# A two-layer graph network on one core: the turned blocks of the attention matrix move from place to place on chip, in halves of a row, instead of through DRAM

## The chip, the core and the metric

The kernel runs on one core of a Trainium2 chip. The core has a matrix engine (TensorE, in the profile PE, with its weight loads as PEld), a vector engine (VectorE, DVE), an engine for functions (ScalarE, ACT), a general engine (GpSimd, POOL) and a queue engine (SyncE, SP) that here issues nearly all DMAs. Sixteen DMA engines do the transfers. The metric is the time of one execution on the device in microseconds (us), median of several runs; lower is better.

## The reference, cut to what matters

There are N = 3327 nodes with 256 features, and a sparse weighted matrix `adj` (3327 x 3327). Layer 0 does two steps of a bilinear attention and of a plain propagation, and layer 1 is an attention over the neighbours with four heads:

```
h = relu(layernorm(x))
# layer 0
R = adj + I;  R = R / R.sum(-1)
Xf = Xa = h;  Z = 0
for n in 0, 1:
    P  = softmax((Xa W1' W2') (Xa W3')')      # 3327 x 3327, dense
    A  = P, in each row the largest entries up to a sum of 0.9, normalised
    Xf = R @ Xf;  Xa = A @ Xa
    Z += Xf @ U1[n]' + Xa @ U2[n]'
x = x + layernorm(h + Z) * g + b
# layer 1
hp = relu(layernorm(x)) @ W                    # 4 heads of 64
e  = leaky_relu(s_i + d_j) where adj > 0, else -inf
x  = x + elu(softmax(e) @ hp)
```

All is float32. The dense product `A @ Xa` is the part that the change touches.

## The kernel before, in words

Nodes are cut into 26 tiles of 128 (3328 places). Layer 0 goes through the 26 tiles of rows twice (steps n = 0 and 1); "a row" below means such a row of tiles, 128 x 3328 numbers called `e`. Layer 1, the neighbour stage, goes over four blocks of 832 columns, and in each over the 26 tiles.

What happens to one row of `e`:

- `logits` (L904) are PE products into PSUM, and `exps` (L919 to L922) writes their exponentials to `e`. It stores them so that each group of 256 columns holds two tiles interleaved.
- `count` (L956) on ScalarE, `before` and `step` on GpSimd (L960 to L1004) search the threshold of the 0.9. `window` (L1014, L1019), `sort` and `choose` on VectorE settle it.
- `drop` (L1070) on VectorE clears what lies below it, in three pieces of 1024, 1024 and 1279 columns.
- `A @ Xa` needs `e` transposed as the stationary operand. `turn_blocks` (L1082) transposes each 32 x 32 block in place with VectorE's stream transpose, piece by piece, three a row. The blocks then have to change places. `put_blocks` (L1086) writes a piece to the DRAM tile `blocks`, and `get_blocks` (L1091) reads it back with block row and block column exchanged, four DMAs a piece, one for each 32 partitions. So a row has 3 puts and 12 gets.
- `attend_blocks` (L1098) makes the 26 products into the PSUM tile `acca`, and `attended` (L1102) scales them out on ScalarE. `finish1` or `finish2` then projects the result for the next step, or closes layer 0 and prepares layer 1.

Beside this runs the full product `R @ Xf` (class `Full`, L1117 loads, L1123 products): seven loads of `adj` a tile (the tile `at`, four buffers), 26 products into `accf`. In layer 1 `load` (L1678) fetches `adj`, `mask` (L1688, L1689) makes a 0/1 mask from it on ScalarE, `exponents` (L1700) on VectorE the unnormalised attention, and `product` (L1716) and `sums` (L1730) on PE the results.

The order of the work is written by a planner. Every piece of work is a `plan.put(engine, length, rank, function, needs=..., take=..., give=..., lag=...)`: the engine that issues it, a time in us, a rank (the lower goes first), what it waits for, which buffers it takes and gives back, and how long after it its result may be used. `Plan.order` plays this through with one queue for each engine, and the program is issued in the order that comes out. On the chip each engine then works off its own list in that fixed order, and semaphores hold it where a result or a buffer is not there yet. The numbers of buffers stand in the dictionary handed to `Plan` and in `BUFS`: `e` 4 and `e5` 1 (a row of `e` in the tile `qq`, for 10 of the 52 rows), `et` 3 and `f` 3. `attention` and `search` set up the pieces of a row. VectorE's turn and SP's moves have ranks just below that row's; full products of step 0 have the rank 2 + 1.3 t for tile t, those of step 1 have 31 + t.

Small users of the buffers that the change touches: `weights`, `layer1_loads`, `layer1_scores`, the copies in `stats` (L826) and the masks use `et`; `Full.copy`, `Full.take` and the fetch of x1 (L1822) use `f`.

Of the kernel before, what the change touches and what calls it, by code (L numbers as in the profile page):

```python
# [10 lines left out]
F32 = mybir.dt.float32  # L11
# [4 lines left out]
ALU = mybir.AluOpType  # L16
# [31 lines left out]
PART = 1024  # L48
PIECE_AT = [PART * (k // 5) + 205 * (k % 5) for k in range(PIECES)] + [N]
# [4 lines left out]
BUFS = dict(kk=2, e=4, sc=6, f=3, xa=2, xt=2, kq=3, ystage=2, base=1, mv=4, cum=2)  # L54
# [532 lines left out]
def fast(  # L587
# [58 lines left out]
    with ExitStack() as l0:  # L646
# [5 lines left out]
        etpool = l0.enter_context(tc.tile_pool(name="etpool", bufs=3))  # L652
# [17 lines left out]
        blocks = spill.tile([NT // 2, P, 2 * P], F32, name="blocks")  # L670
# [27 lines left out]
        def weights():  # L698
            held = {}
            w1 = etpool.tile([P, 4, P], F32, name="et")  # L700
# [49 lines left out]
        def layer1_loads():  # L750
# [4 lines left out]
            a_all = etpool.tile([P, H, 2 * FH], F32, name="et")  # L755
# [4 lines left out]
            return g_all, b_all, wa, a_all  # L760

        def layer1_scores(wa, a_all):

            prod = etpool.tile([P, 2, H, FH], F32, name="et")
            for k in range(2):
                for a in range(2):
                    V.tensor_mul(
                        prod[:, 0],
                        wa[:, k, : H * FH].rearrange("p (h f) -> p h f", h=H),
                        a_all[:, :, a * FH : (a + 1) * FH],  # L770
                    )
                    lo = H * FH + a * H
                    V.tensor_reduce(wa[:, k, lo : lo + H], prod[:, 0], AX.X, ALU.add)
# [35 lines left out]
        def stats(n, lo, hi, rank, needs, scaled):  # L809
# [13 lines left out]
            def copy(held, m):  # L823
                qg = etpool.tile([P, 4, P], F32, name="et").rearrange("p a b -> p (a b)")
                held["qg"] = qg[:, : 3 * (2 * DA + 1)].rearrange("p (a b) -> p a b", a=3)
# [11 lines left out]
            for t0 in range(lo, hi, 2):  # L837
                held, m = {}, min(2, hi - t0)
                a = plan.put("PE", 0.25 * m, rank, product, held, t0, m, needs=[needs, scaled], take=["px"])
                a = plan.put("ACT", 0.45, rank, copy, held, m, needs=[a], take=["et"], give=["px"])  # L840
                ends.append(plan.put("DVE", 0.35 * m + 0.2, rank, square, held, t0, m, needs=[a], give=["et"]))
# [23 lines left out]
        plan = Plan(dict(rows=1, mvs=3, pl=2, px=2, acca=1, accf=1, et=3, at=4, y=1, e2=2, ec=1, mask=2, e5=1, qg=2, **BUFS))  # L865
# [4 lines left out]
        class Row:  # L870
# [7 lines left out]
            def __init__(self, n, i):  # L878
                self.n, self.i, self.pl, self.pt, self.et = n, i, {}, {}, {}
# [197 lines left out]
            def part(self, g):  # L1077
                return self.e[:, g * PART : (g + 1) * PART if g < 2 else NP]

            def turn_blocks(self, g):  # L1080
                part = self.part(g).rearrange("p (g s t) -> p g t s", s=P, t=2)
                V.transpose(part, part)  # L1082

            def put_blocks(self, g):
                src = self.part(g).rearrange("p (g w) -> p g w", w=2 * P)
                nc.sync.dma_start(blocks[4 * g : 4 * g + src.shape[1]].rearrange("g p w -> p g w"), src)  # L1086

            def get_blocks(self, g, o):
                to = self.part(g)[o * P // 4 : (o + 1) * P // 4].rearrange("p (c w) -> p c w", w=P // 2)
                src = blocks[4 * g : 4 * g + to.shape[1] // 4, :, o * P // 2 : (o + 1) * P // 2]  # L1090
                nc.sync.dma_start(to, src.rearrange("g (b s) w -> s (g b) w", b=4))  # L1091

            def attend_blocks(self, js):
                for j in js:
                    if j == 0:
                        self.acc = ps_a.tile([P, D], F32, name="acca")
                    lhs = self.e[:, j // 2 * 256 : (j // 2 + 1) * 256].rearrange("p (q t) -> p t q", t=2)[:, j % 2, :]
# [420 lines left out]
        def attention(row, rank, total, drops, right):  # L1518
            a = None
            come = []  # L1520
            for g in range(3):
                b = plan.put(
                    "DVE", 1.17 if g < 2 else 1.44, rank - 1.001, row.turn_blocks, g, needs=[drops[g]]
                )
                b = plan.put("SP", 0.5, rank - 1.0, row.put_blocks, g, needs=[b], lag=8.0)
                b = plan.put("", 0.0, -90.0, lambda: None, needs=[b], lag=0.0)
                come.append(
                    [plan.put("SP", 0.6, rank - 1.0, row.get_blocks, g, o, needs=[b], lag=5.5) for o in range(4)]
                )
            for j in range(0, NT - 2, 4):  # L1530
                js = range(j, j + 4 if j < 20 else NT)
                a = plan.put(
                    "PE", 0.432 * len(js), rank, row.attend_blocks, js, needs=[come[j // 8], a, right],
                    take=["acca"] * (j == 0), give=[own_e[row.n][row.i]] * (j == 20),
# [28 lines left out]
        def attend_neighbours(rows, ends, done, fulls):  # L1563
# [80 lines left out]
            for b in range(4):  # L1644
# [14 lines left out]
                for j in range(NT):  # L1659
# [22 lines left out]
                    def mask(held=held, off=off):  # L1682
                        m = etpool.tile([P, 4, P], F32, name="et").rearrange("p a b -> p (a b)").bitcast(BF16)
                        m = held["mask"] = m[:, :W]
# [54 lines left out]
                    own = ["et", "mask"]  # L1739
                    if b == 0 and j < 2:  # L1740
                        loads, own = plan.put("SP", 0.2, rank, load_first, needs=[opened[0]], lag=4.0), []
                        m_ = plan.put("ACT", 1.8, rank, mask_first, needs=[loads])
# [198 lines left out]
        for n in range(STEPS):  # L1941
# [30 lines left out]
            if n == 0:  # L1972
# [21 lines left out]
                def layer1():  # L1994
# [7 lines left out]
                    "DVE", 3.7, base + 5.0, lambda: layer1_scores(late["wa"], late["a"]), needs=[a], take=["et"],  # L2002
                    give=["et", "et"],
# [75 lines left out]
```

## Time and profile before

| | us |
|---|---|
| three runs | 2112.4, 2110.24, 2112.68; median 2112.4 |
| the profiled execution | 2112.06 |
| its span, first to last instruction | 2110.3 |
| PE busy | 2033.4 |
| VectorE busy | 1693.6 |
| ScalarE busy | 1297.6 |
| GpSimd busy | 1028.4 |

| from the page | |
|---|---|
| mean granted clock of PE | 0.992 |
| packets, bytes, mean rate | 637551, 361.61 MB, 171 GB/s |
| share of the DMA engines taken by SP's queue | 72.8% |
| bytes read from HBM, and written | 254.39 MB, 104.58 MB |
| puts `blocks<-e` and `blocks<-qq` | 84 + 20 of 512 KB, 42 + 10 of 640 KB |
| gets `e<-blocks` and `qq<-blocks` | 336 + 80 of 128 KB, 168 + 40 of 160 KB |

The profile is of one execution. A busy time counts the time in which an engine had an instruction of its own at work; waiting and issuing DMAs are not in it, so SP has no busy time of its own, and its DMAs are listed with the time that their issue took. Matmuls overlap, and a busy PE need not be PE at its peak. The span falls into a start (to about 100 us), step 0 (to about 780 us), step 1 (to about 1630 us) and the neighbour stage with the output (to 2110 us). Where the waits of an engine are listed, the name behind the arrow is the instruction or DMA whose end came last before the engine went on.

### The profile page before, as it was taken

How to read it: one execution, taken by the hardware profiler on the slowest of the kernel's cores; microseconds unless marked ns; L12 is line 12 of the kernel's file. 1: busy time of each engine (PE TensorE's matmuls, PEld its weight loads, DVE VectorE, ACT ScalarE, POOL GpSimd, SP SyncE). 2: the span in 40 equal slices, each digit the busy share in tenths (PEclk: the TensorE clock that was granted, in tenths of full speed). 3: DMA queues.
4: the chain of work that ended last, by engine and by line, in shares of the span. 5: the costliest groups of instructions: out<-in, count | busy, mean ns of one | idle time of the engine just before them, and what ended most of it. 6: DMA issues, size and time to landing. Idle time of an engine off the chain costs nothing. (4 is left out here: it accounts for less than half of the span.)

```text
span 2110.3 us, 33982 instructions
## 1 busy us (share of the span) xinstructions
PE 2033.4 (96%) x10519; PEld 1398.5 (66%) x10519; DVE 1693.6 (80%) x3768; ACT 1297.6 (61%) x2630; POOL 1028.4 (49%) x2222
## 2 busy tenths in 40 slices
PE   8999999999999889999999999999888999999997
PEld 6477778777787777778878787777776333333332
DVE  5579899887987734788778888888787989999894
ACT  4776685577656307873777777776552447464642
POOL 4367676566665404777577767777672000000001
PEclk9999999999999999999999999999999999999999
DMA  3189889888888975999879898887899444444340
GB/s 95 52 190 212 187 199 216 187 199 190 191 207 180 216 174 161 195 211 220 171 180 200 180 215 188 197 202 175 187 231 203 120 132 138 132 136 119 117 123 27
DMA packets 637551, 361.61 MB, mean 171 GB/s; under 512 B 373706, under 2 KB 590320, under 8 KB 637360
## 3 DMA queue, kind: packets, MB, share of 16 engines
q1 hardware_dynamic: 636464, 359.13, 72.8%
q8 instruction: 86, 1.41, 0.3%
q14 instruction: 105, 0.86, 0.1%
q10 hardware_dynamic: 896, 0.21, 0.0%
HBM read 254.39 MB, written 104.58 MB: 170 GB/s over the span
## 5 line engine op out<-in xcount | busy, mean ns | idle before, releaser
L1098 PE MATMUL acca<-rhs,e 128*128 128x256 f32 x2184 | 489.6, 381 | 18.1 <-DMA e<-blocks 7.0
L956 ACT ACTIVATE junk<-e,sc 128x3327 fp8e5<-128x3327 f32 x147 | 450.8, 3066 | 54.4 <-POOL sc L993 53.0
L1098 PEld LDWEIGHTS acca<-rhs,e 128*128 128x128 f32 x2184 | 425.6, 197 | 70.3 <-issue 13.8
L1123 PE MATMUL accf<-main,at 128*128 128x257 f32 x1352 | 322.2, 387 | 13.0 <-DMA at<-in_adjt_dram 6.7
L1123 PE MATMUL accf<-c,at 128*128 128x256 f32 x1352 | 311.8, 385 | 17.4 <-DMA at<-in_adjt_dram 9.0
L1123 PEld LDWEIGHTS accf<-main,at 128*128 128x128 f32 x1352 | 252.0, 192 | 75.2 <-issue 18.3
L1123 PEld LDWEIGHTS accf<-c,at 128*128 128x128 f32 x1352 | 254.7, 192 | 69.6 <-DMA at<-in_adjt_dram 11.9
L1019 DVE MAX8 cands<-y 128x8 f32<-128x205 f32 (+1 forms) x832 | 242.7, 361 | 3.7
L1014 DVE SCALAR_TENSOR_TENSOR y<-e,sc 128x1639 f32<-128x1639 f32 x84 | 167.3, 1991 | 68.2 <-POOL sc L1004 67.1
L1879 POOL TENSOR_TENSOR qq<-qq 128x256 f32<-128x256 f32 x4 | 2.9, 728 | 432.6 <-ACT qq L1875 432.6
L1716 PE MATMUL pl<-e,main 128*64 128x416 f32 x1024 | 191.6, 517 | 0.0
L1689 ACT ACTIVATE et<-at 128x448 bf16<-128x448 f32 (+1 forms) x204 | 112.2, 550 | 127.6 <-DVE e L1700 71.7
L919 ACT ACTIVATE e<-pl 128x1024 f32<-128x1024 f32 x126 | 137.6, 1099 | 65.7 <-PE pl L904 64.1
L904 PE MATMUL pl<-kt,qg 64*128 64x512 f32 (+1 forms) x832 | 173.7, 536 | 2.8 <-ACT e L919 2.8
L1082 DVE STREAM_TRANSPOSE e<-e 128x1024 f32<-128x1024 f32 (+1 forms) x126 | 168.6, 1338 | 7.1 <-POOL sc L993 0.5
L1070 DVE SCALAR_TENSOR_TENSOR e<-e,thr 128x1024 f32<-128x1024 f32 (+1 forms) x126 | 171.0, 1357 | 1.5 <-issue 0.4
L1716 PEld LDWEIGHTS pl<-e,main 128*64 128x64 f32 x1024 | 69.3, 137 | 110.5 <-issue 95.7
L1688 ACT ACTIVATE at<-at 128x448 f32<-128x448 f32 (+1 forms) x204 | 110.6, 542 | 45.3 <-DMA at<-in_adjt_dram 44.0
L1700 DVE SCALAR_TENSOR_TENSOR e<-c,low,et 128x832 f32<-128x832 f32 x128 | 129.4, 1070 | 8.1 <-issue 6.2
L1700 DVE SCALAR_TENSOR_TENSOR e<-qq,low,et 128x832 f32<-128x832 f32 x120 | 121.8, 1077 | 10.6 <-ACT et L1689 3.8
L904 PEld LDWEIGHTS pl<-kt,qg 64*128 64x128 f32 x832 | 71.4, 186 | 88.1 <-issue 74.7
L1102 ACT ACTIVATE xa<-acca,sc 128x256 f32<-128x256 f32 x52 | 24.2, 466 | 158.3 <-PE acca L1098 158.3
(547 smaller groups left out, 3436.6 us busy)
## 6 DMA issues: line engine op xcount, KB each, us to landing
at<-in_adjt_dram SPq DMA_DIRECT2D x414, 256.0 KB
blocks<-e SPq DMA_DIRECT2D x84, 512.0 KB
e<-blocks SPq DMA_DIRECT2D x336, 128.0 KB
blocks<-e SPq DMA_DIRECT2D x42, 640.0 KB
e<-blocks SPq DMA_DIRECT2D x168, 160.0 KB
at<-in_adjt_dram SPq DMA_DIRECT2D x102, 192.0 KB
blocks<-qq SPq DMA_DIRECT2D x20, 512.0 KB
qq<-blocks SPq DMA_DIRECT2D x80, 128.0 KB
```

Source lines behind the costliest of these rows:

```text
L904: T.matmul(pl[:, lo : lo + m], qg[self.n, self.i // 4][half, self.i % 4, :], kt[half, 512 * k : 512 * k + m], start=True, stop=True,)
L919: S.activation(to, pl.rearrange("p (g t q) -> p g t q", g=4, t=2), AF.Exp, accum_out=sums[k])
L956: S.activation(junk[:, :N], self.e[:, :N], fn, bias=t, scale=-1.0, accum_out=dst, saturate=False)
L1014: V.scalar_tensor_tensor(self.y[:, : hi - lo], self.e[:, lo:hi], self.up, self.e[:, lo:hi], ALU.is_lt, ALU.mult, accum_out=(self.h0, self. ...
L1019: V.max(self.cands[:, a * PIECES // 2 + k, :], self.y[:, at[k] - lo : at[k + 1] - lo])
L1070: V.scalar_tensor_tensor(piece, piece, self.thr[:, at : at + 1], piece, ALU.is_gt, ALU.mult)
L1082: V.transpose(part, part)
L1098: T.matmul(self.acc, lhs, rhs[self.n][:, j, :], start=(j == 0), stop=(j == NT - 1))
L1123: T.matmul(self.acc[:, : self.w], self.at[j // JC][:, j % JC, :], self.src[:, j, : self.w], start=(j == 0), stop=(j == NT - 1),)
L1689: S.activation(to, src, AF.Sign)
L1700: V.scalar_tensor_tensor(held["e"][:, k, :], extra["both"][b % 2][:, k, :], low[:, j, k : k + 1], held["mask"], ALU.max, ALU.mult,)
L1716: T.matmul(q["acc"][a][k * FH : (k + 1) * FH, c, :C], main[:, j, h * FH : (h + 1) * FH], held["e"][:, h, c * C : (c + 1) * C], start=(j == 0),
```

## The change

- VectorE turns a row's blocks in two halves, of 1792 and 1536 columns, in place of three pieces. The first half follows the second drop, the second the third.
- The DRAM tile `blocks`, the puts and the gets are gone. A new buffer of 128 x 1792 (the tile `et`, now one buffer of that size in place of three of 512 columns) takes the first half: `move(0, q)` issues four DMAs, which carry the blocks of 32 source partitions to four places in it. `move(1, q)` then carries the second half into the columns of `e` where the first half stood: four DMAs, all into the same 32 partitions. A row has 32 such DMAs, each of 32 partitions with 7 or 6 runs of 256 bytes.
- `attend_blocks` reads the first 14 tiles from `et` and the last 12 from the front of `e`. Its pieces are cut accordingly; the piece with tiles 12 and 13 gives `et` back.
- The small users of `et` go elsewhere: the copies of `stats` take an `f` buffer, masks take the tile `junk` (two places, the same two `mask` tokens as before), and layer 1's `a` and the products made from it share the one `et`. `f` has two buffers in place of three.

The core of the diff:

```diff
-BUFS = dict(kk=2, e=4, sc=6, f=3, xa=2, xt=2, kq=3, ystage=2, base=1, mv=4, cum=2)
+BUFS = dict(kk=2, e=4, sc=6, f=2, xa=2, xt=2, kq=3, ystage=2, base=1, mv=4, cum=2)
...
-        etpool = l0.enter_context(tc.tile_pool(name="etpool", bufs=3))
+        etpool = l0.enter_context(tc.tile_pool(name="etpool", bufs=1))
...
             def copy(held, m):
-                qg = etpool.tile([P, 4, P], F32, name="et").rearrange("p a b -> p (a b)")
-                held["qg"] = qg[:, : 3 * (2 * DA + 1)].rearrange("p (a b) -> p a b", a=3)
+                qg = small.tile([P, H * FH + 2 * H], F32, name="f", bufs=BUFS["f"])
+                held["qg"] = qg[:, : 2 * (2 * DA + 1)].rearrange("p (a b) -> p a b", a=2)
...
+            def half(self, h):
+                return self.e[:, h * HALF : HALF if h == 0 else NP]
+
+            def turn_blocks(self, h):
+                half = self.half(h).rearrange("p (g s t) -> p g t s", s=P, t=2)
+                V.transpose(half, half)
+
+            def move(self, h, q):
+                if (h, q) == (0, 0):
+                    self.first = etpool.tile([P, HALF], F32, name="et")
+                src = self.half(h).rearrange("p (g o w) -> p g o w", o=4, w=P // 2)
+                to = (self.e if h else self.first)[:, : src.shape[1] * 2 * P]
+                to = to.rearrange("p (g b w) -> p g b w", b=4, w=P // 2)
+                for k in range(4):
+                    o, b = (k, q) if h == 0 else (q, k)
+                    nc.sync.dma_start(to[o * 32 : (o + 1) * 32, :, b, :], src[b * 32 : (b + 1) * 32, :, o, :])
...
-                    lhs = self.e[:, j // 2 * 256 : (j // 2 + 1) * 256].rearrange("p (q t) -> p t q", t=2)[:, j % 2, :]
+                    g = j // 2 * 2 * P
+                    lhs = self.first[:, g : g + 2 * P] if g < HALF else self.e[:, g - HALF : g - HALF + 2 * P]
+                    lhs = lhs.rearrange("p (q t) -> p t q", t=2)[:, j % 2, :]
...
-            for g in range(3):
-                b = plan.put(
-                    "DVE", 1.17 if g < 2 else 1.44, rank - 1.001, row.turn_blocks, g, needs=[drops[g]]
-                )
-                b = plan.put("SP", 0.5, rank - 1.0, row.put_blocks, g, needs=[b], lag=8.0)
-                b = plan.put("", 0.0, -90.0, lambda: None, needs=[b], lag=0.0)
-                come.append(
-                    [plan.put("SP", 0.6, rank - 1.0, row.get_blocks, g, o, needs=[b], lag=5.5) for o in range(4)]
-                )
+            for h in range(2):
+                b = plan.put("DVE", 1.98 if h == 0 else 1.72, rank - 1.001, row.turn_blocks, h, needs=[drops[h + 1]])
+                a, own = b, []
+                for q in range(4):
+                    a = plan.put(
+                        "SP", 1.55, rank - 1.0, row.move, h, q, needs=[b, a, come[0][q] if h else None], take=["et"] * (h + q == 0), lag=3.5
+                    )
+                    own.append(a)
+                come.append(own)
...
-                    def mask(held=held, off=off):
-                        m = etpool.tile([P, 4, P], F32, name="et").rearrange("p a b -> p (a b)").bitcast(BF16)
-                        m = held["mask"] = m[:, :W]
+                    def mask(j=j, held=held, off=off):
+                        m = held["mask"] = extra["m"][:, j % 2, :]
...
-                    own = ["et", "mask"]
+                    own = ["mask"]
```

## The prediction, made before the changed kernel was run

> **What bounds the kernel now.** I read the page's busy times first, then the slices, then stretches of the span, and last what TensorE (PE) waits for.
>
> ```profile
> PE 2033.4 (96%) x10519; PEld 1398.5 (66%) x10519; DVE 1693.6 (80%) x3768; ACT 1297.6 (61%) x2630; POOL 1028.4 (49%) x2222
> ...
> PEclk9999999999999999999999999999999999999999
> DMA  3189889888888975999879898887899444444340
> ```
>
> PE is busy for 2033.4 of 2110.3 us. Its instructions do not change, so whatever the change gains has to come out of the 77 us in which PE is idle, and a little from the clock (0.992 granted on the mean). The DMA digits show the second thing that is nearly full: through both attention steps (about 100 to 1620 us) the 16 engines are 80 to 90% busy. The stretches of the span tell where the idle time of PE lies (columns: length, then busy time of PE, weight loads, VectorE, ScalarE, GpSimd; granted clock; DMA share; GB/s):
>
> ```profile
> 200.00:300.00 100.00, 99.48 (x459) 77.88 (x459) 89.09 (x233) 68.82 (x129) 69.24 (x138) 1.00 0.93 201
> ...
> 700.00:760.00 60.00, 51.17 (x224) 42.02 (x225) 39.75 (x110) 12.79 (x16) 16.92 (x38) 0.98 0.92 199
> ...
> 1400.00:1500.00 100.00, 94.56 (x437) 75.43 (x434) 82.84 (x219) 72.92 (x145) 70.73 (x156) 1.00 0.82 186
> 1500.00:1600.00 100.00, 88.59 (x383) 73.68 (x382) 81.66 (x186) 45.63 (x84) 67.50 (x128) 0.95 0.88 201
> ```
>
> In the middle of step 0 PE is full (3.6 us idle from 200 to 700). It idles 13 us where step 0 ends (700 to 800), 7 us from there to 1000, 13.5 us from 1000 to 1500, 17 us from 1500 to 1650, and 22 us in the first 200 us and the last 110 us, which the change does not touch. What PE waited for over the whole span (us in total, times, longest):
>
> ```profile
> PE accf L1123 <- DMA at<-in_adjt_dram: 15.7, 8, 3.8
> PE acca L1098 <- DMA e<-blocks: 7.0, 11, 1.5
> PE accf L1123 <- ACT main L1137: 5.6, 3, 2.9
> PE acca L1730 <- ACT xa L1102: 4.0, 1, 4.0
> ...
> PE acca L1098 <- DMA qq<-blocks: 1.2, 3, 0.4
> ```
>
> So 23.9 us of the idle time ended with a DMA: 15.7 with a load of adj for the full product, 8.2 with the way through DRAM itself. The rest ended with ScalarE, VectorE and GpSimd, which the change leaves as they are. From about 1650 us on DMA is under half busy and PE has no idle time until 2060; no gain is to be had there.
>
> **What goes: the way through DRAM.** A row of e has 3328 columns. Three puts (L1086) write it in 128 x 13 = 1664 packets of 1 KB, twelve gets (L1091) bring it back in 128 x 52 = 6656 packets of 256 B. The trace's packet records, grouped by size, give 52 ns for a 1 KB packet and 28 ns for a 256 B one (5th to 95th percentile 18 to 47). Over 16 engines that is 1664 x 52 / 16 = 5.4 us for the puts and 6656 x 28 / 16 = 11.7 us for the gets. Rows follow each other every 25.5 us in step 0 (first transposes of row 0 at 102.1, of row 25 at 740.8) and every 29.9 us in step 1 (843.6 and 1592.1). At a share of 0.89 the engines work 22.7 us a row in step 0; the two kinds are 17.1 of them, so all else is 5.6.
>
> The new 32 moves are again 6656 packets of 256 B. No row shows such a packet read on chip. I take the same 28 ns, since the write side is the same (32 partitions, 256 B runs), and keep 18 and 47 ns as ends: 7.5 to 19.6 us a row. With 28 ns a row is 5.6 + 11.7 + 0.2 (17 more completions on 16 engines of 12 ns) = 17.5 us of 25.5: the share falls from 0.89 to about 0.69. That is the gain's source, and its size: a get took 0.9 us of all engines (512 x 28 / 16), a move takes 0.4, so an adj load queued behind them waits half as long.
>
> **What comes: issues on SyncE's queue (SP).**
>
> ```profile
> L1091 SPq DMA_DIRECT2D e<-blocks x504: 303/507/3138, 110.1 to 1616.4; - x168
> L1086 SPq DMA_DIRECT2D blocks<-e x126: 359/377/1047, 103.3 to 1604.0; - x126
> ```
>
> Median issue is 0.38 us for a put and 0.51 for a get, the means 0.39 and 0.70. In the queue's records the DMAs count on eight semaphores in turn, and a long issue is one that waits for the DMA eight places earlier: the get at 321.84 us takes 2.2 us, until the one issued at 316.74 has landed, 7.3 us after its issue. So the surplus over the median is the full engines' doing and shrinks with them. A row's 15 issues cost 9.5 us of SP now, and 0.05 us between each. For a move I take 0.42 us, between the put and the uncongested get; ends 0.33 (an adj load's lower rows) and 0.70. 32 x (0.42 + 0.05) = 15.0 us against 9.5 + 0.8 = 10.3. SP's DMAs fill 53.9% of 200 to 700 us, 13.7 us a row, so the rest is 4.2 (4.5 with the gaps), and SP goes to 19.5 of 25.5 us, 77%. It is not full, but what queues behind a blocked move (the adj loads, which feed the full products) has less room. The plan books 1.55 us for four moves, 0.39 each, so SP will run late against it. I price this at +6 us over 52 rows, from 0 to +45.
>
> The moves wait for the turned half (VectorE), and the first of a row for the single buffer that the first half's products (PE) must have left. Behind that move in SP's queue stand adj loads. The buffer is held for 16 moves (7.5 us), a landing (2 to 3 us) and 14 tiles at 0.45 us (6.3): some 17 us of a 25.5 us row, so it decides nothing unless PE comes 8 us late, and then PE is busy. The second half's moves wait for the first half's reads of the same partitions, which were issued 13 or more DMAs earlier, so eight in flight already cover it.
>
> **What moves.** VectorE turns 1792 and 1536 columns in place of 1024, 1024 and 1280. The rows 1.248 and 1.543 us give 0.07 + 1.15 us per 1000 columns: 2.13 + 1.84 = 3.97 in place of 4.04 us. Nothing. The first data leave later (after the second drop) but the wait of put upon get is gone. Today the last transpose of a row ends 23 to 25 us before its last product, in the last row 28.1 (1599.1 to 1627.2). After: 32 issues from the first half's end, which lies 3.4 us before the second's: 15.0 - 3.4 + 2.5 for the landing + 12 x 0.45 = 19.5 us. Rows end some 4 to 8 us sooner. Where full products fill PE this is worth nothing; at the end of step 1, where the neighbour sums wait 4.0 us for the last row (L1730), I take -3, ends 0 and -10.
>
> The stats' copies and x1 share two f buffers (three before), and masks keep two places (the plan always allowed two, but three buffers let ScalarE run ahead). In the neighbour stage PE has no idle time from 1650 to 2000 and e is seven buffers deep, which hides a mask late by a few tenths; taken as 0, ends 0 and +6.
>
> **A rule that speaks against it.** The Trainium skill, "DMA: Bandwidth & Descriptors", section "Rules for kernel authors", says that transfers under 64 KB pay mostly overhead and should be joined; a move is 56 or 48 KB, a get was 128 or 160. By that page's fixed 2 us a DMA, 32 in a row one after another would be an estimated 64 us and every row would be late. The trace here has eight in flight, gets issued 0.7 us apart and landing 7.3 us later, so I do not count it so; whether short moves on chip keep that pace no run here shows yet.
>
> **The sum.** Adj waits: two thirds of 15.7 go, -10 (0 to -15.7; the two longest, 3.8 and 2.9 us, follow gets in SP's queue). Waits for the blocks: half of 8.2, -4 (0 to -8.2; some become waits for moves). End of step 1: -3. SP: +6. Together -11. The profiled execution took 2112.06 us, 1.8 more than its span and 0.3 under the median of the runs: 2112.06 - 11 = 2101.
>
> **Rivals.**
> (1) SP, or the engines, become the bound: slower. If a move's issue keeps the gets' mean of 0.70 us, a row needs 4.5 + 32 x 0.75 = 28.5 us of SP, 3 more than step 0's row, and 30.7 in step 1 (6.7 of other issues and gaps there, 52% of 29.9 us less 9.5, and 0.6 for gaps), 0.8 more. Step 0's excess is filled with full products that are due later; step 1's is not, 0.8 x 26 = 21 us, and with 8 for blocked loads 2140. It decides from 0.61 us an issue ((25.5 - 4.5) / 32 - 0.05). For it: 32 issues on a queue already 53% in use. Against: the median get, 0.51, is below it. The engines give the same from 47 ns a packet ((25.5 - 5.6 - 0.2) x 16 / 6656).
> (2) Nothing: the 256 B packets remain, PE's waits were only 1% of the span, and the new order of all engines gives back what they lose: 2112.
> (3) All of it: every DMA wait and the end's idle time go, -24 and -5: 2083.
> (4) The one buffer: if products of the first half run late, SP stands at the row's first move and adj loads with it, as it stood 36 us at one place today (L746, for products); at 0.2 us a row +10, 2122.
>
> **How the numbers follow.** Forecast (2092 to 2108) 0.40; rival 3 (below 2092) 0.13; rival 2 (2108 to 2117) 0.14; rivals 1 and 4 0.20 and 0.13. A difference under 0.2% (4.2 us) cannot be told from none here. So faster 0.53, same 0.14, slower 0.33. Low is rival 3's 2083; high 2135 takes in rival 4 and most of rival 1, leaving some 0.15 out.
>
> **What would show it.** Right: DMA share of about 0.7 in both steps, 256 B packets near 28 ns, move issues near 0.42 us, PE's waits for adj loads a few us in all, last transpose to last product below 21 us. Wrong: issues above 0.6 us, SP's waits for the first half's products in tens of us, or more PE waits for adj loads than 15.7 us.

## The result: 2463.9 us, 16.7% slower

| | before | after |
|---|---|---|
| median, fastest and slowest of the runs (us) | 2112.5 (2110.2 to 2113.6) | 2463.9 (2461.5 to 2467.0) |
| span of the profiled execution | 2110.3 | 2459.6 |
| PE busy | 2033.4 | 2143.6 |
| mean granted clock of PE | 0.992 | 0.939 |
| packets, MB moved by DMA | 637551, 361.61 | 565175, 273.12 |
| MB written to HBM | 104.58 | 15.98 |

The ratio is 1.1666 (95% interval 1.1645 to 1.1686). The forecast was 2101, the range 2083 to 2135, so it missed by far and on the other side. The span grew by 349.3 us: 110.2 of them are PE being busy longer with the same 10519 products, 239.1 are PE being idle.

### The profile page after: what moved, and what is told of

Its sections match the earlier page's. It is cut to its first block, busy times and chain, and to the rows that moved or that the text cites. A ratio compares the mean times of both kernels' runs of the same rounds, so it can differ in the third digit from the quotient of the medians.

```text
span 2459.6 us, 34912 instructions
## 1 busy us (share of the span) xinstructions
PE 2143.6 (87%) x10519; PEld 1468.3 (60%) x10519; DVE 1686.5 (69%) x3705; ACT 1301.1 (53%) x2641; POOL 988.3 (40%) x2222
## 2 busy tenths in 40 slices
DMA packets 565175, 273.12 MB, mean 111 GB/s; under 512 B 387851, under 2 KB 517937, under 8 KB 564977
## 3 DMA queue, kind: packets, MB, share of 16 engines
HBM read 165.79 MB, written 15.98 MB: 74 GB/s over the span
## 5 line engine op out<-in xcount | busy, mean ns | idle before, releaser
L1103 PE MATMUL acca<-rhs,et 128*128 128x256 f32 x1456 | 373.0, 419 | 111.3 <-DMA et<-e 65.8
L1103 PEld LDWEIGHTS acca<-rhs,et 128*128 128x128 f32 x1456 | 312.2, 217 | 170.9 <-issue 109.0
L1103 PE MATMUL acca<-rhs,e 128*128 128x256 f32 x1008 | 274.4, 434 | 105.2 <-DMA e<-e 52.4
L1128 PE MATMUL accf<-c,at 128*128 128x256 f32 x1352 | 317.2, 391 | 43.1 <-DMA at<-in_adjt_dram 39.6
L1128 PEld LDWEIGHTS accf<-c,at 128*128 128x128 f32 x1352 | 260.9, 196 | 92.4 <-DMA at<-in_adjt_dram 44.6
L1103 PEld LDWEIGHTS acca<-rhs,e 128*128 128x128 f32 x1008 | 224.4, 226 | 149.8 <-issue 64.1
L1694 ACT ACTIVATE junk<-at 128x448 bf16<-128x448 f32 (+1 forms) x204 | 112.5, 551 | 171.5 <-DVE e L1705 105.3
L1084 DVE STREAM_TRANSPOSE e<-e 128x1792 f32<-128x1792 f32 x84 | 161.0, 1917 | 5.0
L1135 POOL TENSOR_TENSOR at<-at,ident 128x128 f32<-128x128 f32 x52 | 25.0, 481 | 293.1 <-DMA at<-in_adjt_dram 141.0
L1705 DVE SCALAR_TENSOR_TENSOR e<-c,low,junk 128x832 f32<-128x832 f32 x128 | 129.2, 1074 | 5.1 <-issue 3.2
```

Source lines behind the costliest of these rows:

```text
L1084: V.transpose(half, half)
L1103: T.matmul(self.acc, lhs, rhs[self.n][:, j, :], start=(j == 0), stop=(j == NT - 1))
L1128: T.matmul(self.acc[:, : self.w], self.at[j // JC][:, j % JC, :], self.src[:, j, : self.w], start=(j == 0), stop=(j == NT - 1),)
L1705: V.scalar_tensor_tensor(held["e"][:, k, :], extra["both"][b % 2][:, k, :], low[:, j, k : k + 1], held["mask"], ALU.max, ALU.mult,)
```

## The profile after, beside that of before

The page of the kernel after, busy times and slices:

```profile
PE 2143.6 (87%) x10519; PEld 1468.3 (60%) x10519; DVE 1686.5 (69%) x3705; ACT 1301.1 (53%) x2641; POOL 988.3 (40%) x2222
...
PEclk9999999999989899999999989899898999999999
DMA  2244555554445455445544545444445554444341
```

The DMA digits were 8 and 9 and are 4 and 5. What the change was made for has come: the 16 engines, nearly full before, are about half free. But all engines are busy for a smaller share than before, so the time must go into waits for something that is in no list of busy engines. Two stretches of the span, at the same places as before (columns as before: PE, weight loads, VectorE, ScalarE, GpSimd, clock, DMA share, GB/s), show it:

```profile
200.00:300.00 100.00, 86.91 (x367) 66.33 (x368) 73.15 (x174) 52.57 (x99) 50.58 (x116) 0.93 0.52 112
...
1400.00:1500.00 100.00, 83.22 (x346) 66.23 (x346) 65.13 (x182) 55.54 (x100) 56.72 (x126) 0.90 0.49 109
```

PE lost 13 us of every 100 in the middle of step 0, where it had been full, so the loss is spread over all rows. From the first transposes of rows 0 and 25, and of rows 26 and 51, a row takes 31.5 us in step 0 and 37.3 in step 1, against 25.5 and 29.9; 25 x 6.0 + 25 x 7.3 = 333 us, nearly the whole loss. What PE waited for:

```profile
PE acca L1103 <- DMA e<-e: 77.8, 26, 7.4
PE acca L1103 <- DMA et<-e: 65.8, 24, 5.8
PE accf L1128 <- DMA at<-in_adjt_dram: 42.1, 11, 8.1
PE acca L1103 <- DMA kqs<-kq: 23.3, 6, 4.4
PE acca L1103 <- DMA et<-qq: 19.9, 6, 5.4
PE acca L1103 <- DMA qq<-qq: 19.3, 6, 5.2
```

L1103 is the products of a row, which need no DMA but the moves of its blocks; so where another DMA is named (`kqs<-kq`), I read it as only the last to be counted. The six lines are 248 us, against 23.9 for the waits that ended with a DMA before: 224 of the 239 us of new idle time. SP's issues for the moves (columns: count, then shortest, median and longest issue in ns):

```profile
L1094 SPq DMA_DIRECT2D et<-e x672: 585/607/1752, 106.1 to 1955.1; - x168
L1094 SPq DMA_DIRECT2D e<-e x672: 585/604/2056, 116.8 to 1965.5; - x168
```

0.607 us, where I took 0.42. The shortest and the median lie under 4% apart, so it is no backlog, as with the gets (0.30 and 0.51), but a fixed price. With the gap of 0.045 a row needs 32 x 0.65 = 20.8 us of SP; the plan books 12.4. The timeline of SP around row 10 (start, length):

```profile
394.88 10.56 SPq L1122 DMA_DIRECT2D at<-in_adjt_dram  x4
405.53 10.38 SPq L1094 DMA_DIRECT2D et<-e  x16
416.33 11.64 SPq L1094 DMA_DIRECT2D e<-e  x16
...
429.19 1.82 SPq L1122 DMA_DIRECT2D at<-in_adjt_dram  x4
```

and PE in the same time:

```profile
418.23 7.97 PE L1103 MATMUL acca<-rhs,et 128*128 128x256 f32 x28 [1.89 <-DMA e<-e]
429.75 5.55 PE L1103 MATMUL acca<-rhs,e 128*128 128x256 f32 x18 [3.55 <-DMA kqs<-kq]
```

First SP stands among four adj loads for 10.6 us. Row 10 has been turned since 400.5, but its moves begin at 405.5, and PE's list has the row's products next and waits 1.9 and 3.6 us for the two halves. Then no adj load leaves for 24 us. Two queues with a fixed order hold each other up: over the span SP waits 367.8 us for PE to give back an adj buffer (236.1 before, when SP had room to spare), and the moves on which PE waits stand behind. SP's waits, after and before:

```profile
SPq L1122 <- PE accf L1128: 367.8, 142, 9.1
SPq L1117 <- PE accf L1123: 236.1, 172, 6.7
```

This circle is read from the timeline; that the price in the plan sets it off is what e1 and e14 show.

The clock makes it dearer. The clock's records show half the clock for 36.9 us in 7 stretches before and for 301.9 us in 58 stretches after, nearly all of 3.4 or 6.8 us and behind gaps of PE; gaps over 1.5 us were 14 and are 78. Half of the 265 us more, 132, is the most that this can add to PE's busy time; 110 were added. Outside these stretches PE is busy for 192 ns a product in both kernels; of the products that begin inside them (554, before 79) each keeps it busy for 416 ns, and these account for the 110. The Trainium skill, "TensorE: Matmul & The Clock Gate", Part 1, says that the clock falls to half after an idle window of about 3.4 us. The lengths here agree; but stretches already follow gaps of 1.9 us (at 419.0 and 681.8 us), and there the runs decide.

## The experiments

In the expectations Q is the theory of SP's queue (the moves' issue costs more than the plan books, and adj loads stand behind them; where a Q' appears, that the queue is too short even when booked); L, and from e5 on E, is the theory of the single buffer and the landing; S that of the small users with fewer buffers; H that of the cut in halves. Each run has its own runs of the kernel before on the same chip, and ratios are to those. e4 and e8 only add DMAs behind the end of the program, and their whole time is not compared.

| | us | ratio to before, 95% | clock |
|---|---|---|---|
| e1: after, moves booked at 0.65 us | 2219.7 | 1.0525 (1.0492 to 1.0558) | 0.979 |
| e2: before, small users as after | 2105.5 | 0.9983 (0.9964 to 1.0002) | 0.993 |
| e3: before, turned in halves, through DRAM | 2145.3 | 1.0179 (1.0152 to 1.0206) | 0.985 |
| e5: e1, each move a piece, adj loads first | 2144.7 | 1.0178 (1.0157 to 1.0199) | 0.986 |
| e6: e1, row's products first | 2215.8 | 1.0520 (1.0498 to 1.0543) | 0.975 |
| e7: e1, adj loads from ScalarE | 2346.9 | 1.1136 (1.1109 to 1.1164) | 0.956 |
| e9: before, 12 unbooked issues a row more | 2145.4 | 1.0180 (1.0160 to 1.0199) | 0.989 |
| e10: the same, booked | 2120.0 | 1.0059 (1.0040 to 1.0078) | 0.987 |
| e11: whole row on chip, 16 moves, 3 e buffers | 2245.0 | 1.0655 (1.0635 to 1.0674) | 0.977 |
| e12: before, 3 e buffers | 2120.3 | 1.0068 (1.0044 to 1.0093) | 0.992 |
| e13: before, 24 unbooked issues a row more | 2406.6 | 1.1398 (1.1351 to 1.1445) | 0.951 |
| e14: e5, moves booked at 0.39 us | 2482.6 | 1.1772 (1.1741 to 1.1803) | 0.939 |
| e15: last 1280 columns on chip, adj loads first | 2083.7 | 0.9892 (0.9871 to 0.9913) | 0.994 |
| e16: before, adj loads first | 2125.4 | 1.0099 (1.0072 to 1.0125) | 0.989 |
| e17: e15, adj loads at their old place | 2116.1 | 1.0048 (1.0029 to 1.0066) | 0.990 |
| e18: e17 with 1536 columns on chip | 2137.3 | 1.0138 (1.0115 to 1.0162) | 0.984 |

**e1, the moves booked at what they take.**

```
-  plan.put("SP", 1.55, rank - 1.0, row.move, h, q, ...
+  plan.put("SP", 2.6, rank - 1.0, row.move, h, q, ...
```

> The changed kernel, with 2.6 us booked in the plan for four moves in place of 1.55 (measured: 4 x (0.607 + 0.045)); nothing else differs. Theory Q (SyncE's queue: 32 issues of 0.65 us are 21 us a row, the plan books 12.4, so every row runs 8.6 us late and the adj loads stand behind an unbroken run of moves): with the price known the loads get places in time and a good part of the 351 us goes, 2200 to 2330 us, and PE's waits for moves fall to under half of their 183 us. Theory Q' (the queue is simply too short for 32 issues, booked or not): 2420 to 2480. Rival L (the way on chip itself is slow to land, or the single buffer holds it): no change, 2440 to 2480.

One number in the plan gives back 244 of the 351 us: 2219.7 (by the ratios, 5.2% of the 16.7% are left). PE's waits for moves fall from 183 to 45 us. No DMA and no product is other than in the kernel after; only the order is. What is left shows in SP's timeline, where all moves of a row still go in one block and PE waits 11.1 us for adj from 967.4 on:

```profile
954.75 10.39 SPq L1094 DMA_DIRECT2D et<-e  x16
965.25 10.37 SPq L1094 DMA_DIRECT2D e<-e  x16
975.72 1.97 SPq L1122 DMA_DIRECT2D at<-in_adjt_dram  x4
```

**e2, the small users alone.** In the kernel before: `f` with two buffers, the copies of `stats` in `f`, the masks in `junk`.

> The kernel before, with only the small users moved as the change moves them: f with two buffers in place of three, the stats' copies in f, the masks in two places of the junk tile. Blocks still go through DRAM in three pieces. Theories Q, Q' and L: within 10 us of before, 2103 to 2123. Rival S (the small users cost the time, by copies and masks that come late): 2200 us or more.

No loss (0.9983, 0.9964 to 1.0002). That part of the prediction holds.

**e3, the halves alone.** In the kernel before: two turns, puts of 1792 and 1536 columns, two puts and eight gets a row, products cut as after.

> The kernel before, with the turn in two halves of 1792 and 1536 columns and the blocks still through DRAM: 2 puts and 8 gets a row in place of 3 and 12 (10 issues in place of 15). Theory Q and Q': halves do no harm, and five issues fewer free some 2.5 us of SP a row, 2085 to 2125 us. Rival H (cutting the row in halves, so that the first products wait for 14 tiles, is what makes PE wait): 2200 us or more.

Slower by 38 us, which I had not expected: PE's waits for adj go from 15.7 to 38.0 us in 20 places. Why is not shown. A larger get (224 or 192 KB in place of 128 or 160) may stand longer in front of an adj load; and the gets' issues take 0.94 us in the mean where 0.6 is booked, so with the gap some 3.1 us a row are unknown to the plan, against 1.8 before. It is far from rival H's 2200, so the halves by themselves are not the cause of the 351; what part they have in it on chip was not separated.

**e4, what the issue costs alone.** The kernel before with 56 DMAs behind its end, on a quiet SP: the move's shape, the same without crossing partitions, one run of 1792 B, 128 partitions, to DRAM and back.

> The kernel before, and behind it 56 DMAs on an otherwise quiet SP queue, eight of each shape: 32 partitions x 7 x 256 bytes on chip to other partitions (a move), the same to the same partitions, 32 partitions x 1792 bytes in one run on chip, 128 partitions x 7 x 256 bytes on chip, 32 partitions x 7 x 256 bytes to DRAM, the same from DRAM, 128 partitions x 7 x 256 bytes to DRAM. Theory Q: the move's 0.607 us is the price of issuing this shape and shows here too, 0.58 to 0.63. Rival L: it is backlog, and alone it is 0.33 to 0.45. Which of the shapes is cheap tells what the price hangs on: on 32 partitions against 128, on two on-chip sides, or on the cut in 256-byte runs.

The move's shape takes 0.608 us with no other work on the chip, the single run 0.590, the same without crossing partitions 0.607. So it is neither contention nor the 256 B cut nor the crossing. But 128 partitions of 7 runs take more, 0.67 to 0.69 us for the first three and 0.91 to 1.03 for the rest (on chip here; to DRAM much the same):

```profile
L2053 SPq DMA_DIRECT2D i_to<-i_src x8: 666/957/1027, 2121.0 to 2127.3; - x8
```

**e8, twelve shapes**, in the same place.

```
+        for k in range(min(6, 256 // parts)):
+            lo = parts * k % P
+            nc.sync.dma_start(z[lo : lo + parts, :, parts * k // P % 2, :], a[lo : lo + parts, :, parts * k // P % 2, :])
```

> The kernel before with twelve groups of DMAs behind it on the quiet SP, one shape each, to see what the 0.607 us of a move's issue hangs on. If it is the number of partitions, every 32-partition group takes 0.6, the 16-partition one less and the 64-partition one about the same or more. If it is the size (56 and 48 KB, no power of two), the groups of 8, 4 and 16 runs and of one run of 1 or 2 KB take 0.33 to 0.5. If it is that both sides lie on chip, the two groups that read from DRAM take 0.4 to 0.5 and the on-chip ones 0.6. The group of the move's own shape repeats 0.6.

The groups (32 partitions if not named; "i_p32r" holds the groups of 8, 4, 16 and 7 runs together, "r1w" those of one run of 1 or 2 KB; "far" reads from DRAM):

```profile
L2051 SPq DMA_DIRECT2D i_p32r<-i_src x24: 585/622/1406, 2111.3 to 2156.4; - x24
L2051 SPq DMA_DIRECT2D i_p32r1w<-i_src x12: 588/589/597, 2123.3 to 2130.3; - x12
L2051 SPq DMA_DIRECT2D i_p16r<-i_src x6: 597/598/633, 2130.9 to 2134.2; - x6
...
L2051 SPq DMA_DIRECT2D i_p32r8far<-i_off x6: 448/449/616, 2146.1 to 2148.7; - x6
...
L2051 SPq DMA_DIRECT2D i_p1r<-i_src x6: 587/588/603, 2157.0 to 2160.2; - x6
```

None of the three guesses holds as put. Up to 64 partitions neither their number nor the size matters much: one run of 256 B in one partition takes 0.588, 128 KB in 32 partitions 0.63, 64 partitions 0.64. So from place to place on chip an issue of these groups costs some 0.6 us, whatever it carries; e4's 128 partitions cost more, and eight DMAs at the start of the kernel before less (`qg<-kq`, 64 partitions of one run of 512 B: 0.46 to 0.55). With a side in DRAM it is 0.45 here for 8 runs, 0.33 to 0.38 for an adj load and a put, but 0.60 to 0.63 for 7 and 16 runs (e4 and this run), so that rule is not whole; what decides between those stays open. For this change it is enough: a move of 56 or 48 KB costs SP no less to issue than one of 256 B, and the change made 32 issues of 15. The rule that I weighed and set aside, from the Trainium skill's "DMA: Bandwidth & Descriptors", "Rules for kernel authors" (join transfers under 64 KB), pointed the right way, though not by the landing with which I argued. The same page says under "Issuing engines are not separate DMA queues" that the time to initiate a DMA is usually small relative to the DMA itself; here it is not: a move's 224 packets take 224 x 23.8 ns / 16 = 0.33 us of the 16 engines and 0.65 of SP.

**e5, adj loads between the moves.** Each of the 32 moves is a piece of 0.65 us, and adj loads rank 40 places earlier.

```
-  plan.put("SP", 0.4, rank, f.load, q, needs=[after], take=["at"], lag=4.0)
+  plan.put("SP", 0.4, rank - 40.0, f.load, q, needs=[after], take=["at"], lag=4.0)
```

> The changed kernel with each of the 32 moves of a row a piece of its own, booked at the 0.65 us that it takes with its gap, and the adj loads of the full products ranked 40 places earlier, so that SP issues one between two moves as soon as a buffer is free. Theory Q (SP's queue: moves cost more than booked, and adj loads stand behind unbroken runs of them): the full products' waits for adj fall from the 26.6 us of e1 to under 8, and the time from 2219.7 to 2150 to 2190. Theory E (the single buffer for the first half is held too long by late products, and the moves of the next row stand behind it): the waits for adj may fall, but rows 29 to 36 stay 90 us long and the time stays at 2205 to 2225.

2144.7: below even the better end for Q. The pieces and the loads' place came in one edit and are not separated. The waits for adj are 10.7 us, a little more than expected; those for moves take their place:

```profile
PE acca L1102 <- DMA e<-e: 31.7, 10, 13.8
PE accf L1127 <- DMA at<-in_adjt_dram: 10.7, 9, 2.8
```

SP is as good as full here: from 200 to 800 us its issues fill 88 to 91 of every 100 us, and with the gaps (150 x 0.05) some 97, while PE is 96% busy from 200 to 700. Rows take 26.2 and 30.7 us. That makes SP the likely bound; but e3's halves cost as much (38 us) through DRAM, and this kernel has them too, so how its 39 us above the kernel before divide is not shown. That the time lies at the 2140 of rival 1 is partly luck: that price was worked out with 0.70 us an issue.

**e14, the same with the old booking** (0.39 us in place of 0.65, nothing else).

> e5 (each move its own piece, adj loads ranked ahead) with the old booking, 0.39 us a move in place of 0.65. If the booking carries the gain: 2380 to 2480. If the place of the adj loads carries it: 2140 to 2200. Theory Q takes the first: rows are let in faster than SP can move them, whatever the order in the queue.

2482.6, just above the range for the booking. So the booking alone carries 338 us, and the place of the adj loads saves nothing as long as the plan has the price wrong.

**e6, the row's products first.**

```
-  "PE", 0.432 * len(js), rank, row.attend_blocks, js, ...
+  "PE", 0.432 * len(js), rank - 40.0, row.attend_blocks, js, ...
```

> The changed kernel with 2.6 us booked for four moves (as in e1) and a row's products of attention ranked 40 places earlier, so that PE takes them ahead of all full products as soon as their half has landed, and the single buffer is given back at once. Theory E: the long rows 29 to 36 go, the time falls from 2219.7 by 40 to 70, to 2150 to 2180. Theory Q: PE only changes the order of what it has, adj loads still come late, 2205 to 2230.

2215.8 against 2219.7: theory E falls. In the kernel after, too, SP waited only 6.3 us for PE's products before a move. Rows 29 to 33 take 75 to 78 us from the last transpose to the last product where they took 91 to 101 in e1, and rows 35 to 47 some 30 where they took 31 to 60: the edit does shorten them, and the time does not follow.

**e7, adj loads from ScalarE's queue** (`nc.scalar.dma_start`, booked on ScalarE).

> The changed kernel with 2.6 us booked for four moves (as in e1), and the adj loads of the full products issued by ScalarE instead of SyncE: seven issues of some 0.33 us leave SP a row. Theory Q: SP has 3 us of a row more and no adj load stands behind a move: 2150 to 2190 and waits for adj under 8 us, unless ScalarE (61% busy before) makes them wait. Theory E: 2205 to 2225.

2346.9, the other way. The waits of SP show why:

```profile
SPq L1094 <- DMA at<-in_adjt_dram: 258.8, 140, 7.8
```

The moves now wait 258.8 us for adj loads that they need for nothing: DMAs of both queues count on the same few semaphores in turn, so an issue on SP waits for a load that ScalarE sent. The run says nothing on Q; it says that a second issuing engine is not free here.

**e9 and e10, issues without moves.** The kernel before, blocks through DRAM, and behind each get a DMA of 8 KB from a constant to a place of its own that nobody reads; e10 books it (1.25 us for both in place of 0.6).

```
   nc.sync.dma_start(to, src.rearrange("g (b s) w -> s (g b) w", b=4))
+  nc.sync.dma_start(idle_[next(idle_at)], ident[32 * o : 32 * o + 32, :64])
```

> The kernel before, its blocks still through DRAM, with one more DMA behind each get (twelve a row, 624 in all, 8 KB each from a constant to a place of its own in DRAM that nobody reads), which the plan does not book. At some 0.6 us and a gap each they take 7.8 us of SP a row and next to nothing of the 16 engines (32 packets each). Theory Q (issue time on SP that the plan does not know of is by itself enough for the loss): 2180 to 2400, PE's waits for adj and blocks over 60 us. If the loss of the changed kernel needs the moves themselves (their landing, the single buffer, the on-chip sides): 2105 to 2125.

> The same twelve additional DMAs a row in the kernel before, booked: 1.25 us for a get with its companion in place of 0.6. Theory Q: the plan spreads the rows, and what stays is SP's lack of room (4.5 + 10.3 + 7.8 = 22.6 of 25.5 us): 2110 to 2160, well below the unbooked one. If booking does not matter the two are alike within 0.5%.

2145.4 and 2120.0. I had expected 2180 to 2400 for e9. Two things make it milder: the gets fell from 0.70 to 0.47 us in the mean between the small DMAs, so a row's unbooked time is 12 x (0.47 + 0.52 + 0.10) - 7.2 = 5.9 us against 12 x 0.75 - 7.2 = 1.8 before, 4.1 more and not 7.8; and SP, at about 19 of 25.5 us, could still catch up. Booking brings back 25 of the 37 us.

**e13, twice as many** (two behind each get, unbooked).

> As e9, with two unbooked small DMAs behind each get, 24 a row: 4.5 + 1.3 (puts) + 12 x 0.52 + 24 x 0.57 = 25.7 us of SP in a row of 25.5, against 7.2 booked for the gets and 0 for the rest. Theory Q with a threshold (unbooked time costs little while SP can catch up, and much when the queue is full): 2300 to 2550, PE's waits for blocks and adj over 100 us together, granted clock below 0.96. If the price only adds up in proportion, twice e9's loss: 2175 to 2190. If the loss belongs to the moves themselves: under 2190 as well.

2406.6: eight times e9's loss for twice its issues, with the picture of the kernel after (clock 0.951, 74 gaps of PE over 1.5 us, rows of 31.0 and 35.6 us), and no block moved on chip:

```profile
PE acca L1102 <- DMA idle<-ident: 130.9, 57, 4.8
PE accf L1127 <- DMA at<-in_adjt_dram: 46.6, 18, 5.2
PE acca L1102 <- DMA e<-blocks: 26.3, 12, 3.9
```

(`idle<-ident` is again only the last DMA counted; L1102 waits for gets.) By the working of e9 the unbooked time is 24 x 0.53 + 12 x 0.50 - 7.2 = 11.5 us a row. So a loss of this size needs two things together: issue time that the plan doesn't know of, and so much of it that SP has no room left at the pace of the plan. It needs neither the moves nor the buffer. That booking would bring this kernel back too was not run.

**e11 and e12, sixteen moves.** VectorE turns a whole row out of `e` into one buffer of a row's length, in an order in which each pair of quarters is one run of 3328 B, and 16 moves bring it back. There is room for it only in place of one `e` buffer; e12 is the kernel before with three.

> Blocks on chip, but with half the issues: VectorE turns a whole row out of e into one buffer of a row's length, laid out so that each pair of quarters is one run of 3328 B, and 16 moves a row (each booked at 0.65 us) bring it back to e. The buffer takes the place of one of the four e buffers, so this is compared with e12. SP's share of a row is 4.5 + 16 x 0.65 = 14.9 us, as in the kernel before. Theory Q: the loss goes, within 1% of e12 on either side, and the DMA share falls to about half. If the way on chip itself costs (landing, one buffer held for turn, moves and landing), it stays 40 us or more above e12.

> The kernel before with three e buffers in place of four, blocks through DRAM: what e11's lost buffer costs by itself. Fewer rows are under way; 2110 to 2200. No theory depends on it, it is the base for e11.

2245.0 against 2120.3: missed, and not to be read as I had meant. The new order costs elsewhere: a transpose of 896 columns into it takes 1.94 us where 1024 in place took 1.25, VectorE's busy time rises from 1693.6 to 1834.2, and a weight load with its wide step takes 316 ns where it took 196 (medians). (SP's waits for the turns are no sign: 229.2 us, and 246.2 in e12.) So this run does not decide whether 16 moves by themselves would do; e15 takes 16 moves for a part of a row, without the new order.

**e15 and e16, a part of a row on chip.** Only the last 1280 columns go on chip, in 16 moves of 0.65 us; two parts of 1024 go through DRAM as before; adj loads rank 40 places earlier. e16 has only this last edit, in the kernel before.

```
   for g in range(3):
       b = plan.put("DVE", ..., row.turn_blocks, g, needs=[drops[g]])
+      if g == 2:
+          for k in range(16):
+              a = plan.put("SP", 0.65, rank - 1.0, row.move, k // 4, k % 4, needs=[b, a], take=["et"] * (k == 0), lag=3.5)
```

> Only the last 1280 columns of a row go on chip, in 16 moves booked at 0.65 us each; the first two parts of 1024 go through DRAM as before; adj loads ranked ahead as in e5. SP: 4.5 + 2 x 0.43 + 8 x 0.54 + 16 x 0.65 = 20.1 of 25.5 us, the 16 engines at some 0.8. Theory Q: SP is not full, so no loss like the changed kernel's; 2090 to 2125. If a single on-chip buffer costs by itself, 2140 or more.

> The kernel before with the adj loads ranked 40 places earlier, nothing else: the base for e15 and e5. Its waits for adj are 15.7 us; if their place in the queue is the reason they fall to under 6 us and the time to 2095 to 2105; if the full engines are the reason, 2105 to 2120.

2083.7, better than I expected and faster than both kernels: 0.9892 (0.9871 to 0.9913). SP has 68 to 80 of 100 us in issues through both steps (52 where one passes into the other), the DMA share is 0.78 in 200 to 700 us, PE idles 0.3 us there:

```profile
PE 2026.3 (97%) x10519; PEld 1398.3 (67%) x10519; DVE 1697.5 (82%) x3776; ACT 1291.3 (62%) x2622; POOL 1036.8 (50%) x2222
...
DMA  3177778777778876886776787777786444444441
```

e16 is slower than before by 19 us, against both its theories: its waits for adj fall to 8.1 us, but those for `e<-blocks` rise from 7.0 to 19.9.

**e17 and e18, what e15 owes to what.** e17 takes the early rank of the loads away; e18 then carries 1536 columns in the same 16 moves.

> e15 with the adj loads at their old place in the queue: only the last 1280 columns on chip, 16 moves booked at 0.65 us. Theory Q (the relief of the 16 engines is worth what the prediction gave it, as long as SP has room and the plan knows the price): 2075 to 2100, at or below e15's 2084, since e16 showed that the earlier place costs 19 us in the kernel before. If e15's gain was the loads' place: 2100 to 2115.

> e17 with 1536 columns on chip in the same 16 moves (six runs each instead of five) and 1024 and 768 through DRAM: the same issues on SP, 256 columns less through DRAM. Theory Q: the issue's price does not depend on the size, so the time is that of e17 within 0.5%, the DMA share 0.01 to 0.03 lower.

2116.1 and 2137.3, both against theory Q: there the relief of the engines was to gain without the early loads, and the two runs were to be alike. The part on chip alone doesn't pay (+9 us), the early loads alone don't (+19), both together gain 23. e17's waits for adj are 16.3 us, as in the kernel before, though its DMA share is 0.75, and in e16 they are 8.1 with a share of 0.90; so these waits hang on the loads' place in the queue more than on full engines. Not on it alone: in e18, with the old place, they are 8.8. The loads can go early without making blocks late only where the engines have room: in e15 the waits for adj are 9.7 us and those for moved blocks 2.4. That this is why both together gain is argued, not shown. e18 lies 21 us above e17; there one wait of 12.9 us (for `qg<-kqs`, 1.2 in e17) is new, and those for moves are 19.4 us (6.2 in e17). That a new order of the whole program shifts the time by some 20 us either way is seen in e16 and e18 (in e3 nearly twice that), and their single causes stay open; the 23 us of e15 are measured, but are of that size too.

## Why the prediction was wrong, point by point

- **What bounds the kernel.** Right as far as it went: PE has no spare time. I treated the 77 us of idle time as the limit of any gain, but set no such limit on a loss.
- **The relief of the DMA engines.** Right, and rather too small: 23.8 ns a packet in place of 28, a share of 0.50 and not 0.69 (from 200 to 700 us; 0.50 x 31.5 = 15.8 us a row against 17.5).
- **The move's issue, 0.42 us.** The first wrong size: 0.607. The rows between which I put it, the put (0.38) and the get (0.51), have a side in DRAM. One row of before is on chip on both sides and I overlooked it: the eight `qg<-kq` (L1234), at 0.46 to 0.55 us, all above 0.42. The upper end of 0.70 did hold it. I took the middle of two neighbours because a move is smaller, but for shapes like the move's the issue doesn't go by size (e8).
- **"The plan books 0.39 us each, so SP will run late against it. I price this at +6 us."** This is the step that failed. In the changed kernel itself the booking measures 244 us (e1), with loads first 338 (e14 and e5). I counted SP's time against the row's (77% full), and never asked what the fixed lists of PE and SP do to each other when one item in every row is late by 20.8 - 12.4 = 8.4 us. PE does not go on to other work, because its list was written for a move of 0.39 us. A row's pitch grew by 6.0 and 7.3 us, most of those 8.4. The two wrong sizes belong together: with 0.42 an issue SP would have been 77% full, and e9 shows unbooked time costing 37 us while SP has room; how the 351 us divide between them was not run.
- **Rival 1.** Its mechanism, a full SP, came: the measured 0.607 us lies at its threshold of 0.61. Its price left the booking out. Once the plan knows the price the kernel takes 2144.7 (e5), near its 2140, but partly by luck: with 0.607 in place of 0.70 its own sum for step 1 leaves SP not full (6.7 + 32 x 0.65 = 27.5 of 29.9 us), and e3's halves may have a part in e5's time.
- **Rival 4 and the single buffer.** Rightly priced near nothing (6.3 us of SP's waits in the kernel after; e6).
- **The small users, the turns.** Right: e2; and 2.05 + 1.79 = 3.84 us a row of turns where I had 3.97.
- **"Adj waits: two thirds of 15.7 go."** In the changed kernel they rose to 42.1. The reason is not borne out even where SP has room: e17 has the relief and still waits 16.3 us (e18 8.8). The loads' place in the queue counts as well (e15, e16).
- **The halves.** Counted at nothing; through DRAM they cost 38 us (e3). On chip their part was not separated.
- **The signs named.** Issues above 0.6 us and more than 15.7 us of adj waits both came; SP's waits in tens of us for the first half's products did not.

## What to carry to other kernels

Where a program's order is written out from booked times, a new kind of instruction needs its measured price in the plan before anything is concluded from its time: one wrong number cost 244 us here, or 338 with the loads first, and what is left once it is right some 39 (e5). Count a queue's issues as you count an engine's work, by number and measured price and not by bytes, and look for room at the pace that the plan sets: twelve late issues a row cost 37 us, twenty-four 300. A transfer saved is worth something only as far as the instructions that take its place fit into their queue, so try a part before all, and measure it: one part on chip gained 23 us with early loads (e15) and lost 9 and 30 without (e17, e18).

## What the runs showed of the hardware that I had not expected

- Issuing a DMA from place to place on chip costs SP 0.58 to 0.64 us (medians of e8's groups), from 256 B in one partition to 128 KB in 32; 128 partitions of 7 runs took 0.67 to 1.03 (e4), 64 partitions of one run of 512 B 0.46 to 0.55 (`qg<-kq`). In the kernel after, an adj load from DRAM takes 0.33 when SP stood idle before it, 0.38 right behind another load and 0.54 right behind a move.
- A packet of 256 B on chip takes 23.8 ns in the kernel after (200 to 700 us, DMA share 0.50), one read from DRAM 27.4 before (same stretch, share 0.90).
- In this program the DMAs issued by ScalarE and by SP count on the same eight semaphores in turn, and one engine's issue can wait for the other's transfer (258.8 us in e7).
- PE's clock goes to half for 3.4 or 6.8 us behind gaps from 1.9 us on (not behind every one: 78 gaps over 1.5 us, 58 stretches), so 239 us of idle time brought 110 us of slower products with it.
- VectorE's transpose into a layout with a step of 104 B takes 2.2 ns a column where in place it took 1.2, and a weight load with that step 316 ns for 196.
